# A conditioned attention layer and a GRU: q and k projected by 32-token blocks and heads, turned by VectorE's block transposes

## The chip, the cores and the metric

The kernel runs on one core of a Trainium2 chip. The time is device microseconds (us) of one launch, the median over runs. A core has five engines that run side by side and wait for each other through semaphores: TensorE (PE) multiplies matrices and writes its results to PSUM, eight banks of 128 partitions by 512 float32; VectorE (DVE), ScalarE (ACT) and GpSimd (POOL) compute elementwise on SBUF, the working memory; SyncE (SP) starts DMA transfers. POOL reads and writes SBUF alone here. Everything is float32.

## The reference, cut to what matters

```python
# x (16, 256, 512), cond (16, 512); 16 heads of 32; T = 256 tokens, B = 16
def attention(x, emb, W_emb, b_emb, g_norm, W_qkv, g_q, g_k, W_out):
    scale, shift = jnp.split(emb @ W_emb + b_emb, 2, axis=-1)
    xn = rms_norm(x, g_norm) * (1.0 + scale) + shift
    q, k, v = heads_of(xn @ W_qkv)                  # each (b, h, n, d)
    q, k = rms_norm(q, g_q), rms_norm(k, g_k)       # over d, per head
    attn = softmax(einsum('bhqd,bhkd->bhqk', q, k) * d ** -0.5)
    o = einsum('bhqk,bhkd->bhqd', attn, v)          # back to (b, n, 512)
    return o + o @ W_out

def gru(h, inputs, W_ih, W_hh, b_ih, b_hh):         # one step for each token
    gi, gh = x_t @ W_ih + b_ih, h @ W_hh + b_hh
    r, z = sigmoid(i_r + h_r), sigmoid(i_z + h_z)
    n = tanh(i_n + r * h_n)
    h = (1 - z) * n + z * h

x = x + attention(x, cond, ...)
x = x + gru(cond, x, ...)
```

## The kernel before

The kernel has two stages. The first, the attention of 16 batches, takes about a third of the span; the second is the GRU, 256 steps one after another, and the change doesn't touch its instructions.

**Order.** PE, DVE, ACT and POOL execute in the order in which the source issues instructions (`manual_schedule`, L699); only SP's DMA queue is ordered by a planner. A wait on an engine therefore holds everything that the source issues behind it on that engine.

**Slots.** The attention runs as a hand-made software pipeline (L783 to L788). For each batch b there are four slots, one for each group g of four heads. Each slot starts with `logits` of (b, g), and beside it works on three other things: the exponentials of this group, the end of the group before (`prev`), and a piece of the projection for the next batch m = b+1. In a slot
- `logits` (L302) gives PE eight matmuls 128x256 into the PSUM banks lg0 to lg3, one bank for each head;
- `maxima` (L330, DVE, 4 instructions) and `exps` (L334, ACT, 8) make the unnormalized attn from those banks; `normalize` (L344) takes a reciprocal on DVE and scales the eight halves on POOL, the scale being ready at the end of the slot, so that POOL works at the start of the next;
- `turn(prev)` (L368) transposes attn of the group before on PE, 32 blocks, into the same banks lg0 to lg3, in two halves: lg0 and lg1 first, lg2 and lg3 second. Each half needs its banks read by this slot's exponentials and attn from POOL;
- `put_turned` (L384) copies those banks to SBUF, by letters: "v" a whole bank on DVE, "a" on ACT, "s" a bank on DVE in two halves;
- `weigh(prev)` (L394) multiplies with v, 8 matmuls of 256 columns, into a bank named in the call; `put_weighed` (L410) copies the result o to `oT` on ACT.

**Projection.** `project(b, n, s, ks, a)` (L237) computes q, k or v (s = 0, 1, 2) for token half n (128 tokens) into one bank: for each of four chunks k of the 512 inputs, four matmuls of 32 tokens by 512 columns, each in its own strip of 32 partitions. In PSUM a partition is a token and a column is (head, d). The profile records each of these float32 matmuls twice. Per batch there are 6 such projections; the slots issue them in pieces: slot 0 makes q of half 0 and starts k of half 0, slot 1 ends it and makes q of half 1, slot 2 k of half 1 and the start of v, slot 3 v. Banks A, X, Y, Z hold them, and o in turn.

**From projection to qkT.** `square` (L252, ACT) and `sum_heads` (L260, DVE) give sums of squares per head, `Rsqrt.first` (L158; one DVE step and Ln, Exp on ACT) and `Rsqrt.second` (L165; three small DVE steps) the reciprocal root. `norm_qk` (L268, DVE, two instructions 128x512) scales q and k into SBUF. As logits need d in the partitions, `turn_qk` (L281) transposes both on PE, 16 blocks for each token half, to two PSUM banks, and `put_qk` (L288) copies these to `qkT` while it multiplies by g_q or g_k (`g_cols`; the factor 32 ** -0.5 is in g_q), one bank on DVE and one on ACT. In slot 3 both token halves are turned, one before and one after attn's transposes. `qkT` is one buffer.

**The next x.** `norm_first` (squares on ACT), `norm_apply` (DVE, writes `xs`), `turn_x` (PE, into Y and Z in slot 0) and `put_x` (DVE, in the first batches ACT too) make `xnT`, two batches ahead. `norm_apply` also issues a DMA for a later x.

**Weights.** `we` (W_emb, 2 MB) and later `wih` (W_ih, 3 MB) share a buffer, tag w_a; `wih` is loaded at the start, 16 DMAs on SP behind x of the first batches, W_qkv and W_out, as soon as `we` has been used (L746). `whh` takes the place of W_qkv after the last projection. `last_batch` (L641) does the attention of the last batch with nothing beside it.

Of the kernel before, what the change touches and what calls it, by code (L numbers as in the profile page):

```python
# [8 lines left out]
F32 = mybir.dt.float32  # L9
AF = mybir.ActivationFunctionType  # L10
# [9 lines left out]
def kernel(  # L20
# [42 lines left out]
    ada_s = const.tile([P, KC, B], F32, name="ada_s")  # L63
    g_cols = const.tile([P, 2], F32, name="g_cols")

# [22 lines left out]

    rows = p1.tile([14, P], F32, tag="qkn", name="rows", bufs=4)
    nc.scalar.dma_start(rows[0:8, :], b_emb.rearrange("(m c) -> m c", c=P))  # L90
# [14 lines left out]

    we = wpool.tile([P, KC, 2 * D], F32, tag="w_a", name="we")
    wq = wpool.tile([P, KC, 3 * D], F32, tag="w_b", name="wq")
# [25 lines left out]

    qkT = p1.tile([P, 2, NG, T], F32, name="qkT")
    qT, kT = qkT[:, 0], qkT[:, 1]

# [42 lines left out]
    def norm_first(b, parts=range(NT)):  # L179
        if parts[0] == 0:  # L180
            batches[b].ssx = small.tile([P, NT], F32, tag="ssx", name=f"ssx_{b}")
            batches[b].rs = Rsqrt(batches[b].ssx, D, NT, f"x{b}")
            if b != 2:
                batches[b].xs = p1.tile([P, NT, D], F32, tag="xs", name=f"xs_{b}")
        for n in parts:

            squares = batches[b].xs[:, n, :] if b != 2 else spare(f"squares_{n}")
            nc.scalar.activation(
                squares, x_tiles[b][:, n, :], AF.Square,
                accum_out=batches[b].ssx[:, n : n + 1],  # L190
            )
# [5 lines left out]
    def norm_apply(b, rstd):  # L197
        if b == 2:
            batches[b].xs = p1.tile([P, NT, D], F32, tag="xs", name=f"xs_{b}")
        for n in range(NT):  # L200
            nc.vector.tensor_scalar(
                batches[b].xs[:, n, :], x_tiles[b][:, n, :], rstd[:, n : n + 1],
                None, ALU.mult,
            )
# [14 lines left out]
    def turn_x(b, banks):  # L219
        tps = [tile_ps(f"tpx_{b}_{r}", banks[r], (P, KC, NT, QR)) for r in range(R)]  # L220
        for c in range(KC):
            for n in range(NT):
                turn_block(
                    [tp[:, c, n, :] for tp in tps], batches[b].xs[:, n, c * P : (c + 1) * P]
                )
        return tps
# [10 lines left out]
    def project(b, n, s, ks, a):  # L237
# [12 lines left out]
        return a  # L250

    def square(b, n, s, a):  # L252
        if b == 0:
            sq = spare(f"sq_{b}_{n}_{s}")
        else:
            sq = p1.tile([P, D], F32, tag="sq", name=f"sq_{b}_{n}_{s}")
        nc.scalar.activation(sq, a, AF.Square)
        return sq
# [3 lines left out]

    def put_v(b, n, a, engine=nc.scalar):
        if n == 0:
            batches[b].v = p2.tile([P, NT, D], F32, tag="v", name=f"v_{b}")
        (nc.scalar.copy if engine is nc.scalar else nc.vector.tensor_copy)(batches[b].v[:, n, :], a)

    def norm_qk(b, n, accs, rstd):  # L268
        out = []
        for s in range(2):  # L270
            qk = p1.tile([P, H, DH], F32, tag="qkn", name=f"qkn_{b}_{n}_{s}", bufs=4)
            nc.vector.tensor_tensor(
# [7 lines left out]

    def turn_qk(b, n, normed, banks):  # L281
        tps = [tile_ps(f"tpqk_{b}_{n}_{r}", banks[r], (P, 2, NG, QR)) for r in range(R)]
        for s in range(2):
            for c in range(NG):
                turn_block([tp[:, s, c, :] for tp in tps], normed[s][:, c * P : (c + 1) * P])
        return tps

    def put_qk(n, r, tps, engine):  # L288

        dst = qkT[:, :, :, n * P + QR * r : n * P + QR * r + QR]  # L290
        if engine is nc.scalar:
            for s in range(2):
                nc.scalar.activation(dst[:, s], tps[r][:, s], AF.Copy, scale=g_cols[:, s : s + 1])
        else:
            g = g_cols.unsqueeze(2).unsqueeze(3).to_broadcast([P, 2, NG, QR])
            nc.vector.tensor_tensor(dst, tps[r], g, ALU.mult)

# [18 lines left out]
    def add_logits(w, heads):  # L316
        for i in heads:
            w.lg[i] = ps_lg.tile([P, NT, T], F32, tag=f"lg{i}", name=f"lg_{w.b}_{w.g}_{i}")
        for n in range(NT):
            for i in heads:  # L320
                r = slice(i * DH, (i + 1) * DH)
                nc.tensor.matmul(  # L322
                    w.lg[i][:, n, :],
                    qT[r, w.g, n * P : (n + 1) * P],
                    kT[r, w.g, :],
                    start=True,
                    stop=True,
                )
# [100 lines left out]
    def slot0(b, w, prev, st):  # L429
        m = b + 1  # L430
        if b == 0:


            v = project(b, 1, 2, range(KC), "X")
            put_x(1, 0, st.tpx)
# [4 lines left out]
            norm_apply(2, batches[2].rs.second())  # L440
            put_v(b, 1, v)
            st.q = project(m, 0, 0, range(KC), "A")
            tp = turn_x(2, "YZ")
# [3 lines left out]
            st.s0.add(0, st.s0.square(0, st.q))  # L447
            st.k = project(m, 0, 1, (0, 1), "X")
            normalize(w)
            return  # L450
        put_v(b, 1, st.v1)
        st.q = project(m, 0, 0, range(KC), "A")
        tpx = turn_x(b + 2, "YZ") if b + 2 < B else None
# [16 lines left out]
    def slot1(b, w, prev, st):  # L470
        m = b + 1
        project(m, 0, 1, (2, 3), st.k)
        st.q1 = project(m, 1, 0, (0, 1, 2), "Z")
        maxima(w, range(HG))
# [3 lines left out]
        put_turned(prev, "vasa")  # L478
        project(m, 1, 0, (3,), st.q1)
        st.s0.add(1, sq)  # L480
        if b + 3 < B:
            norm_first(b + 3, (0,))
        st.s0.rs.first()
        st.s1 = Stats(m, 1)
        st.sq = st.s1.square(0, st.q1)
        weigh(prev, "Y")
        put_weighed(prev)
        st.rstd = st.s0.rs.second()
        normalize(w)

    def slot2(b, w, prev, st):
        m = b + 1
        k = project(m, 1, 1, range(KC), "Y")
        maxima(w, range(HG))
        st.qk0 = norm_qk(m, 0, (st.q, st.k), st.rstd)
        st.v0 = project(m, 0, 2, (0,), "A")
        exps(w, range(HG))
        st.s1.add(0, st.sq)
        sq = st.s1.square(1, k)
        turn(prev)  # L500
        put_turned(prev, "vasa")
        project(m, 0, 2, (1,), st.v0)
        st.s1.add(1, sq)
        if b + 3 < B:
            norm_first(b + 3, (1,))
        st.s1.rs.first()
        if b + 3 < B:
            batches[b + 3].rs.first()
        weigh(prev, "X")
        put_weighed(prev)  # L510
        if b == 0:
# [9 lines left out]
        st.accs = (st.q1, k)  # L521
        st.rstd = st.s1.rs.second()
        normalize(w)

    def slot3(b, w, prev, st):
# [3 lines left out]
        maxima(w, range(HG))  # L529
        qk1 = norm_qk(m, 1, st.accs, st.rstd)  # L530
        tq0 = turn_qk(m, 0, st.qk0, "ZY")
        if b + 3 < B:
            rstd = batches[b + 3].rs.second()
        put_v(m, 0, st.v0, nc.vector)
        exps(w, range(HG))
        put_qk(0, 0, tq0, nc.vector)
        put_qk(0, 1, tq0, nc.scalar)
        turn(prev)
        put_turned(prev, "vava")

        tq1 = turn_qk(m, 1, qk1, "AZ")
        project(m, 1, 2, (3,), st.v1)
        put_qk(1, 0, tq1, nc.vector)
        put_qk(1, 1, tq1, nc.scalar)
        if b + 3 < B:
            norm_apply(b + 3, rstd)
        normalize(w)
        weigh(prev, "Y")
        put_weighed(prev)
# [149 lines left out]
    with tc.manual_schedule(engines=ORDERED):  # L699
# [29 lines left out]
        nc.vector.tensor_copy(cols, tp[:, :14])  # L729
        nc.vector.tensor_scalar(g_cols[:, 0:1], cols[:, 12:13], DH ** -0.5, None, ALU.mult)  # L730
        nc.vector.tensor_copy(g_cols[:, 1:2], cols[:, 13:14])
        load_x(2)
# [44 lines left out]
        put_v(0, 0, v)
        put_qk(0, 0, tq0, nc.vector)
        put_qk(0, 1, tq0, nc.scalar)
        put_qk(1, 0, tq1, nc.vector)  # L780
        put_qk(1, 1, tq1, nc.scalar)

# [233 lines left out]
```

## Time and profile before

| | us |
|---|---|
| median of three runs | 1729.38 (1729.19 to 1732.28) |
| profiled execution, its own time | 1729.55 |
| its span in the profile | 1727.6 |
| attention of batches 0 to 14 (first logits at 32.8, first of the last batch at 573.1) | 540.3 |
| granted TensorE clock | 1.00 |

Busy time of the groups around the change:

| group | count | busy us | mean ns |
|---|---|---|---|
| qkv, PE matmuls 128x512 (L243) | 3072 | 354.7 | 596 |
| tpqk, PE transposes of q and k (L217) | 512 | 22.1 | 226 |
| tpa, PE transposes of attn (L217) | 2048 | 78.9 | 225 |
| qkT copies on ACT 128x256 (L293) | 64 | 27.4 | 487 |
| qkT copies on DVE 128x512 (L296) | 32 | 22.0 | 686 |
| qkn on DVE 128x512 (L272) | 64 | 40.9 | 681 |
| v copies on DVE / ACT 128x512 (L266) | 15 / 17 | 10.2 / 10.7 | 683 / 629 |
| attn scaled on POOL 128x256 (L349) | 510 | 234.1 | 482 |

How to read it: "busy" is the time in which an engine executes, and instructions of one engine overlap at their ends, so that a group's busy time divided by its count is less than the mean duration of one. PE matmuls of four strips run beside each other. An engine's idle time counts only where the chain that ends last goes through it. A line such as `128*32 128x512` gives the rows and columns of PE that are in use, and then partitions by elements of the result.

### The profile page before, as it was taken

To read this page: it belongs to the slowest core of one execution; us is meant where nothing else is said; L and a number is where in the kernel's file an instruction comes from. 1 tells how busy PE (TensorE), PEld (TensorE's weight loads), DVE (VectorE), ACT (ScalarE), POOL (GpSimd) and SP (SyncE) were. 2 spreads that over 40 slices of the span, in tenths; PEclk is the share of its full clock that TensorE was granted. 3 is DMA by queue.
4 is the path that set the end of the run, shared out by engine and by line. 5 is a ranking of instruction groups with operands and counts; after the bars stand their busy time and mean duration, and the time that the engine had idled before them with its cause. 6 is when DMAs were issued, how large, how long until landed. Compare 5 with 4: busy or idle time off the path is not lost.

```text
span 1727.6 us, 95661 instructions
## 1 busy us (share of the span) xinstructions
PE 1709.4 (99%) x42876; PEld 1262.6 (73%) x42876; DVE 1058.1 (61%) x3326; ACT 734.4 (43%) x2678; POOL 317.2 (18%) x773
## 2 busy tenths in 40 slices
PE   8999999999999999999999999999999999999998
PEld 4444444444444698888888888888888888888887
DVE  4777777777776755555555555555555555555554
ACT  4777777777777622222222222222222222222222
POOL 0444334443344400000000000000000000000000
PEclk9999999999999999999999999999999999999999
DMA  8100000000000310000000000000000000000000
GB/s 284 46 14 14 17 24 14 14 15 21 8 2 2 76 34 17 17 22 22 17 17 23 22 17 17 19 24 18 17 18 22 21 17 16 17 10 11 10 16 15
DMA packets 50505, 44.36 MB, mean 26 GB/s; under 512 B 10195, under 2 KB 43327, under 8 KB 50095
## 3 DMA queue, kind: packets, MB, share of 16 engines
q1 hardware_dynamic: 49959, 38.21, 8.0%
q8 instruction: 336, 5.51, 1.3%
q14 instruction: 74, 0.61, 0.1%
q10 hardware_dynamic: 136, 0.04, 0.0%
HBM read 29.79 MB, written 8.39 MB: 22 GB/s over the span
## 4 chain that ended last, share of the span: by engine, by line
PE 84%; DVE 6%; ACT 4%; POOL 2%; DMA 2%; issue 1%; SPq 0%; DVEq 0%; ACTq 0%; POOLq 0%
PE gr L601 25%; PE gz L601 18%; PE qkv L243 13%; PE gn L601 13%; PE o L810 6%; PE tpa L217 2%; POOL attn L349 2%; PE lg L322 2%; DVE attnT L380 2%; ACT attn L338 2%; PE o L402 2%; DVE xnT L235 2%; DMA wih<-in_L_cond_W_ih_dram 1%; PE tpqk L217 1%; DVE ssqk L261 1%
## 5 line engine op out<-in xcount | busy, mean ns | idle before, releaser
L243 PE MATMUL qkv<-wq,xnT 128*32 128x512 f32 x3072 | 354.7, 596 | 4.7 <-ACT oT L413 3.5
L349 POOL TENSOR_SCALAR attn<-attn,rden 128x256 f32<-128x256 f32 x510 | 234.1, 482 | 361.0 <-DVE rden L346 235.1
L932 ACT ACTIVATE r<-trr 128x64 f32<-128x64 f32 x256 | 65.5, 256 | 515.2 <-DVE trr L859 513.4
L601 PE MATMUL gr<-wih,xT 128*32 128x256 f32 x4096 | 268.9, 379 | 0.0
L338 ACT ACTIVATE attn<-lg,neg 128x256 f32<-128x256 f32 x512 | 234.9, 486 | 51.9 <-DVE neg L332 34.3
L859 DVE STREAM_TRANSPOSE trr<-gr 128x128 f32<-128x128 f32 x256 | 81.2, 317 | 274.6 <-PE gr L601 274.6
L243 PEld LDWEIGHTS qkv<-wq,xnT 128*32 128x32 f32 x3072 | 88.3, 109 | 186.4 <-issue 166.4
L938 ACT ACTIVATE n<-n 128x64 f32<-128x64 f32 x256 | 65.7, 257 | 307.9 <-DVE n L937 306.4
L601 PEld LDWEIGHTS gr<-wih,xT 128*32 128x32 f32 x4096 | 135.3, 110 | 83.0
L332 DVE TENSOR_REDUCE neg<-lg 128x2 f32<-128x512 f32 x256 | 159.2, 683 | 26.0 <-PE lg L322 24.8
L859 DVE STREAM_TRANSPOSE trh<-gn 128x128 f32<-128x128 f32 x256 | 81.2, 317 | 116.8 <-PE gn L601 116.8
L810 PE MATMUL o<-oT,wo 128*32 128x256 f32 x1920 | 148.1, 379 | 0.0
L968 POOL TENSOR_TENSOR y<-xT,padded 128x64 f32<-128x64 f32 x128 | 41.2, 322 | 534.2 <-DVE padded L966 534.2
L601 PE MATMUL gr<-whh,padded 128*32 128x128 f32 x4096 | 136.1, 273 | 2.7 <-DVE padded L966 1.4
L601 PEld LDWEIGHTS gr<-whh,padded 128*32 128x32 f32 x4096 | 114.8, 109 | 30.4 <-DVE padded L966 29.9
L601 PE MATMUL gz<-wih,xT 128*32 128x128 f32 x4096 | 135.8, 273 | 0.0
L601 PE MATMUL gn<-whh,padded 128*32 128x128 f32 x4096 | 135.6, 273 | 0.0
L601 PE MATMUL gz<-whh,padded 128*32 128x128 f32 x4096 | 135.6, 273 | 0.0
L601 PE MATMUL gr<-whh,h 128*16 128x128 f32 x4064 | 134.7, 273 | 0.7 <-DVE h L966 0.4
L601 PE MATMUL gz<-whh,h 128*16 128x128 f32 x4064 | 134.6, 273 | 0.0
L601 PE MATMUL gn<-whh,h 128*16 128x128 f32 x4064 | 134.6, 273 | 0.0
L601 PEld LDWEIGHTS gz<-wih,xT 128*32 128x32 f32 x4096 | 117.9, 110 | 21.4
(120 smaller groups left out, 2471.6 us busy)
## 6 DMA issues: line engine op xcount, KB each, us to landing
x<-in_x_dram SPq DMA_DIRECT2D x16, 512.0 KB, 3.5
xin<-in_x_dram SPq DMA_DIRECT2D x256, 32.0 KB, 2.6
out_dram<-osb SPq DMA_DIRECT2D x248, 32.0 KB, 1.7
wq<-in_L_cond_W_qkv_dram SPq DMA_DIRECT2D x4, 768.0 KB
wih<-in_L_cond_W_ih_dram SPq DMA_DIRECT2D x16, 192.0 KB, 6.6
whh<-in_L_cond_W_hh_dram SPq DMA_DIRECT2D x16, 192.0 KB, 6.4
we<-in_L_cond_W_emb_dram SPq DMA_DIRECT2D x4, 512.0 KB, 4.8
wo<-in_L_cond_W_out_dram SPq DMA_DIRECT2D x1, 1024.0 KB, 16.9
```

What stands on the lines that cost most here:

```text
L217: nc.tensor.transpose(dst[r], src[q], ident[q, q])
L235: nc.vector.tensor_scalar(dst, tps[r][:, c], a, s, ALU.mult, ALU.add)
L243: nc.tensor.matmul(a[32 * j : 32 * j + 32, :], batches[b].xnT[:, k, n * P + 32 * j : n * P + 32 * j + 32], wq[:, k, s * D : (s + 1) * D], ...
L332: nc.vector.tensor_reduce(w.neg[:, i, :], w.lg[i], AX.X, ALU.max, negate=True)
L338: nc.scalar.activation(a[:, n, :], w.lg[i][:, n, :], AF.Exp, bias=w.neg[:, i, n : n + 1], accum_out=w.den[:, i, n : n + 1],)
L349: engine.tensor_scalar(w.attn[i][:, n, :], w.attn[i][:, n, :], w.rden[:, i, n : n + 1], 1.0, ALU.mult, ALU.mult,)
L601: nc.tensor.matmul(dst[32 * j : 32 * j + rows], stationary, w[:, k, :].rearrange("p (g j c) -> p j g c", g=3, c=P)[:, j, first::2][:, : ds ...
L810: nc.tensor.matmul(acc[32 * j : 32 * j + 32, :], w[:, k, P * j + 32 * m : P * j + 32 * m + 32], rhs, start=(k == 0), stop=(k == KC - 1),)
L859: nc.vector.transpose(tr.rearrange("p q s b -> p (q s b)"), gate)
L932: nc.scalar.activation(r, turned("r", t, gr[:, 0, :])[:, :, s, :], AF.Sigmoid)
L938: nc.scalar.activation(n, n, AF.Tanh)
L968: (nc.gpsimd if t + 1 < T else nc.vector).tensor_tensor(y[:, :, tl * B : (tl + 1) * B], xTs[grp][:, :, ti, :], h, ALU.add)
```

## The change

It replaces the way in which q and k reach `qkT`.

- A new `project_qk` takes the place of `project` for q and k. One bank now holds 64 tokens of q and k together: partition strip j holds 32 tokens of head j of every group of four heads, and the two column halves i are two blocks of 32 tokens. So there are twice as many matmuls with half the columns each, and the weight columns that one reads are eight pieces of 32.
- `turn_qk` uses VectorE's transpose, which turns each block of 32x32 by itself, from SBUF straight to `qkT`, one instruction of 128x512 for each bank. `qkT` has two buffers, one for each of two batches.
- `put_qk` is gone. g_q, g_k and 32 ** -0.5 are multiplied into one column `g_col`, and `scale_q` scales q alone in place, on POOL (in the first batch on ACT).
- In slot 2 the transposes for token half 0, in slot 3 those for half 1 follow `norm_qk`; the second part of the reciprocal root for half 1 moves from slot 2 to slot 3. v of half 0 is copied by ACT, later. In slot 1 and slot 2 `weigh` and `put_weighed` stand ahead of a square or the next `Rsqrt.first`. In slot 3 o goes to bank Z, and a bank of attn is copied in halves.
- `xs` becomes a part of the buffer w_a behind `we`; `wih` is loaded in slot 1 of batch 13 in the source, and SP's planner puts the first 8 of its 16 DMAs early.
- In the first batch three of four chunks of v for token half 1 are projected ahead of the first logits.

```diff
+    def project_qk(b, n, m, ks, a):
+        if isinstance(a, str):
+            a = tile_ps(f"qk_{b}_{n}_{m}", a)
+        w = wq[:, :, 0 : 2 * D].rearrange("p k (s g j d) -> p k j s g d", s=2, j=HG, d=DH)
+        for k in ks:
+            for i in range(2):
+                t = n * P + 64 * m + 32 * i
+                for j in range(HG):
+                    nc.tensor.matmul(
+                        a[32 * j : 32 * j + 32, i * T : (i + 1) * T],
+                        batches[b].xnT[:, k, t : t + 32],
+                        w[:, k, j],
+                        start=(k == 0 and i == 0),
+                        stop=(k == KC - 1),
+                        skip_group_check=True,
+                    )
+        return a
...
-    def turn_qk(b, n, normed, banks):
-        tps = [tile_ps(f"tpqk_{b}_{n}_{r}", banks[r], (P, 2, NG, QR)) for r in range(R)]
-        for s in range(2):
-            for c in range(NG):
-                turn_block([tp[:, s, c, :] for tp in tps], normed[s][:, c * P : (c + 1) * P])
-        return tps
-
-    def put_qk(n, r, tps, engine):
...
+    def turn_qk(b, n, normed):
+        if n == 0:
+            batches[b].qkT = p1.tile([P, 2 * NG, T], F32, tag="qkT", name=f"qkT_{b}", bufs=2)
+        for m, a in enumerate(normed):
+            t = n * P + 64 * m
+            nc.vector.transpose(
+                batches[b].qkT[:, :, t : t + 64].rearrange("p h (i t) -> p i h t", i=2), a
+            )
+
+    def scale_q(b, n, engine=nc.gpsimd):
+        q = batches[b].qkT[:, 0:NG, n * P : (n + 1) * P]
+        if engine is nc.scalar:
+            nc.scalar.activation(q, q, AF.Copy, scale=g_col)
+        else:
+            engine.tensor_scalar(q, q, g_col, 1.0, ALU.mult, ALU.mult)
...
     def slot1(b, w, prev, st):
...
+        elif b + 3 == B:
+            load_rows(wih, w_ih)
         st.s0.rs.first()
         st.s1 = Stats(m, 1)
-        st.sq = st.s1.square(0, st.q1)
         weigh(prev, "Y")
         put_weighed(prev)
+        st.sq = st.s1.square(0, st.q1)
         st.rstd = st.s0.rs.second()
         normalize(w)

     def slot2(b, w, prev, st):
         m = b + 1
-        k = project(m, 1, 1, range(KC), "Y")
+        k = project_qk(m, 1, 1, range(KC), "Y")
         maxima(w, range(HG))
-        st.qk0 = norm_qk(m, 0, (st.q, st.k), st.rstd)
+        qk0 = norm_qk(m, 0, (st.q, st.k), st.rstd)
+        turn_qk(m, 0, qk0)
+        scale_q(m, 0)
         st.v0 = project(m, 0, 2, (0,), "A")
         exps(w, range(HG))
-        st.s1.add(0, st.sq)
         sq = st.s1.square(1, k)
         turn(prev)
         put_turned(prev, "vasa")
         project(m, 0, 2, (1,), st.v0)
+        st.s1.add(0, st.sq)
         st.s1.add(1, sq)
         if b + 3 < B:
             norm_first(b + 3, (1,))
+        weigh(prev, "X")
+        put_weighed(prev)
         st.s1.rs.first()
         if b + 3 < B:
             batches[b + 3].rs.first()
-        weigh(prev, "X")
-        put_weighed(prev)
...
     def slot3(b, w, prev, st):
...
-        qk1 = norm_qk(m, 1, st.accs, st.rstd)
-        tq0 = turn_qk(m, 0, st.qk0, "ZY")
+        turn_qk(m, 1, norm_qk(m, 1, st.accs, st.s1.rs.second()))
+        scale_q(m, 1)
+        exps(w, range(HG))
+        turn(prev)
+        put_turned(prev, "vasa")
+        put_v(m, 0, st.v0)
+        project(m, 1, 2, (3,), st.v1)
         if b + 3 < B:
-            rstd = batches[b + 3].rs.second()
-        put_v(m, 0, st.v0, nc.vector)
-        exps(w, range(HG))
-        put_qk(0, 0, tq0, nc.vector)
-        put_qk(0, 1, tq0, nc.scalar)
-        turn(prev)
-        put_turned(prev, "vava")
-
-        tq1 = turn_qk(m, 1, qk1, "AZ")
-        project(m, 1, 2, (3,), st.v1)
-        put_qk(1, 0, tq1, nc.vector)
-        put_qk(1, 1, tq1, nc.scalar)
-        if b + 3 < B:
-            norm_apply(b + 3, rstd)
+            norm_apply(b + 3, batches[b + 3].rs.second())
         normalize(w)
-        weigh(prev, "Y")
+        weigh(prev, "Z")
         put_weighed(prev)
...
+        turn_qk(0, 0, qk0)
+        scale_q(0, 0, nc.scalar)
         norm_first(2)
-        qk1 = norm_qk(0, 1, accs[1], s1.rs.second())
-        tq0 = turn_qk(0, 0, qk0, "AX")
-        tq1 = turn_qk(0, 1, qk1, ("lg2", "lg3"))
+        turn_qk(0, 1, norm_qk(0, 1, accs[1], s1.rs.second()))
+        put_v(0, 0, v)
+        scale_q(0, 1, nc.scalar)
         st.tpx = turn_x(1, "YZ")
+        st.v1 = project(0, 1, 2, (0, 1, 2), "X")
```

More of the change, by code (lines that the diff above doesn't have):

```diff
@@ L63 @@
     ada_s = const.tile([P, KC, B], F32, name="ada_s")
-    g_cols = const.tile([P, 2], F32, name="g_cols")
+    g_col = const.tile([P, 1], F32, name="g_col")
     b_rows = const.tile([P, 4, P], F32, name="b_rows")
@@ L86 @@
     ps = ctx.enter_context(tc.tile_pool(name="ps", bufs=1, space=PSUM))
-    rows = p1.tile([14, P], F32, tag="qkn", name="rows", bufs=4)
+    rows = p1.tile([14, P], F32, tag="qkn", name="rows", bufs=2)
     nc.scalar.dma_start(rows[0:8, :], b_emb.rearrange("(m c) -> m c", c=P))
@@ L104 @@
     load_x(0)
-    we = wpool.tile([P, KC, 2 * D], F32, tag="w_a", name="we")
+    w_a = wpool.tile([P, KC * 3 * D], F32, name="w_a")
+    we = w_a[:, 0 : KC * 2 * D].rearrange("p (k n) -> p k n", k=KC)
+    xs = w_a[:, KC * 2 * D : KC * 2 * D + NT * D].rearrange("p (n d) -> p n d", n=NT)
+    wih = w_a.rearrange("p (k n) -> p k n", k=KC)
     wq = wpool.tile([P, KC, 3 * D], F32, tag="w_b", name="wq")
@@ L128, in load_small @@
                 nc.sync.dma_start(h0P[r, q, :], h0T[32 * q : 32 * q + 32, j, :])
-    qkT = p1.tile([P, 2, NG, T], F32, name="qkT")
-    qT, kT = qkT[:, 0], qkT[:, 1]
     def load_rows(dst, w):
@@ L182, in norm_first @@
             batches[b].rs = Rsqrt(batches[b].ssx, D, NT, f"x{b}")
-            if b != 2:
-                batches[b].xs = p1.tile([P, NT, D], F32, tag="xs", name=f"xs_{b}")
         for n in parts:
-            squares = batches[b].xs[:, n, :] if b != 2 else spare(f"squares_{n}")
+            squares = xs[:, n, :] if b != 2 else spare(f"squares_{n}")
             nc.scalar.activation(
@@ L197, in norm_apply @@
     def norm_apply(b, rstd):
-        if b == 2:
-            batches[b].xs = p1.tile([P, NT, D], F32, tag="xs", name=f"xs_{b}")
         for n in range(NT):
             nc.vector.tensor_scalar(
-                batches[b].xs[:, n, :], x_tiles[b][:, n, :], rstd[:, n : n + 1],
+                xs[:, n, :], x_tiles[b][:, n, :], rstd[:, n : n + 1],
                 None, ALU.mult,
@@ L223, in turn_x @@
                 turn_block(
-                    [tp[:, c, n, :] for tp in tps], batches[b].xs[:, n, c * P : (c + 1) * P]
+                    [tp[:, c, n, :] for tp in tps], xs[:, n, c * P : (c + 1) * P]
                 )
@@ L261, in sum_heads, with put_v @@
         nc.vector.tensor_reduce(ss[:, s, :], sq.rearrange("p (h d) -> p h d", d=DH), AX.X, ALU.add)
-    def put_v(b, n, a, engine=nc.scalar):
+    def put_v(b, n, a):
         if n == 0:
             batches[b].v = p2.tile([P, NT, D], F32, tag="v", name=f"v_{b}")
-        (nc.scalar.copy if engine is nc.scalar else nc.vector.tensor_copy)(batches[b].v[:, n, :], a)
+        nc.scalar.copy(batches[b].v[:, n, :], a)
     def norm_qk(b, n, accs, rstd):
@@ L270, in norm_qk @@
         for s in range(2):
-            qk = p1.tile([P, H, DH], F32, tag="qkn", name=f"qkn_{b}_{n}_{s}", bufs=4)
+            qk = p1.tile([P, H, DH], F32, tag="qkn", name=f"qkn_{b}_{n}_{s}", bufs=2)
             nc.vector.tensor_tensor(
@@ L279, in norm_qk @@
         return out
-    def turn_qk(b, n, normed, banks):
-        tps = [tile_ps(f"tpqk_{b}_{n}_{r}", banks[r], (P, 2, NG, QR)) for r in range(R)]
-        for s in range(2):
-            for c in range(NG):
-                turn_block([tp[:, s, c, :] for tp in tps], normed[s][:, c * P : (c + 1) * P])
-        return tps
-    def put_qk(n, r, tps, engine):
-        dst = qkT[:, :, :, n * P + QR * r : n * P + QR * r + QR]
+    def turn_qk(b, n, normed):
[8 more added lines that the diff above has]
+        q = batches[b].qkT[:, 0:NG, n * P : (n + 1) * P]
         if engine is nc.scalar:
-            for s in range(2):
-                nc.scalar.activation(dst[:, s], tps[r][:, s], AF.Copy, scale=g_cols[:, s : s + 1])
-        else:
-            g = g_cols.unsqueeze(2).unsqueeze(3).to_broadcast([P, 2, NG, QR])
-            nc.vector.tensor_tensor(dst, tps[r], g, ALU.mult)
+            nc.scalar.activation(q, q, AF.Copy, scale=g_col)
+        else:
+            engine.tensor_scalar(q, q, g_col, 1.0, ALU.mult, ALU.mult)
     class Group:
@@ L323, in add_logits @@
                     w.lg[i][:, n, :],
-                    qT[r, w.g, n * P : (n + 1) * P],
-                    kT[r, w.g, :],
+                    batches[w.b].qkT[r, w.g, n * P : (n + 1) * P],
+                    batches[w.b].qkT[r, NG + w.g, :],
                     start=True,
@@ L431, in slot0 @@
         if b == 0:
-            v = project(b, 1, 2, range(KC), "X")
+            project(b, 1, 2, (3,), st.v1)
             put_x(1, 0, st.tpx)
@@ L440, in slot0 @@
             norm_apply(2, batches[2].rs.second())
-            put_v(b, 1, v)
-            st.q = project(m, 0, 0, range(KC), "A")
+            put_v(b, 1, st.v1)
+            st.q = project_qk(m, 0, 0, range(KC), "A")
             tp = turn_x(2, "YZ")
@@ L447, in slot0 @@
             st.s0.add(0, st.s0.square(0, st.q))
-            st.k = project(m, 0, 1, (0, 1), "X")
+            st.k = project_qk(m, 0, 1, (0, 1), "X")
             normalize(w)
@@ L451, in slot0 @@
         put_v(b, 1, st.v1)
-        st.q = project(m, 0, 0, range(KC), "A")
+        st.q = project_qk(m, 0, 0, range(KC), "A")
         tpx = turn_x(b + 2, "YZ") if b + 2 < B else None
@@ L461, in slot0 @@
         put_turned(prev, "vava")
-        st.k = project(m, 0, 1, (0, 1), "X")
+        st.k = project_qk(m, 0, 1, (0, 1), "X")
         if tpx:
@@ L471, in slot1 @@
         m = b + 1
-        project(m, 0, 1, (2, 3), st.k)
-        st.q1 = project(m, 1, 0, (0, 1, 2), "Z")
+        project_qk(m, 0, 1, (2, 3), st.k)
+        st.q1 = project_qk(m, 1, 0, (0, 1, 2), "Z")
         maxima(w, range(HG))
@@ L478, in slot1 @@
         put_turned(prev, "vasa")
-        project(m, 1, 0, (3,), st.q1)
+        project_qk(m, 1, 0, (3,), st.q1)
         st.s0.add(1, sq)
@@ L521, in slot2 @@
         st.accs = (st.q1, k)
-        st.rstd = st.s1.rs.second()
         normalize(w)
@@ L729 @@
         nc.vector.tensor_copy(cols, tp[:, :14])
-        nc.vector.tensor_scalar(g_cols[:, 0:1], cols[:, 12:13], DH ** -0.5, None, ALU.mult)
-        nc.vector.tensor_copy(g_cols[:, 1:2], cols[:, 13:14])
+        nc.vector.scalar_tensor_tensor(
+            g_col, cols[:, 12:13], DH ** -0.5, cols[:, 13:14], ALU.mult, ALU.mult
+        )
         load_x(2)
@@ L743 @@
         nc.sync.dma_start(wo, w_out.rearrange("(k p) n -> p k n", p=P))
-        wih = wpool.tile([P, KC, 3 * D], F32, tag="w_a", name="wih")
-        load_rows(wih, w_ih)
         for c in range(KC):
@@ L753 @@
             for i in range(2):
-                accs[n][i] = project(0, n, i, ks, accs[n][i])
+                accs[n][i] = project_qk(0, n, i, ks, accs[n][i])
         v = project(0, 0, 2, range(KC), "lg0")
@@ L771 @@
         s1.rs.first()
+        turn_qk(0, 0, qk0)
+        scale_q(0, 0, nc.scalar)
         norm_first(2)
-        qk1 = norm_qk(0, 1, accs[1], s1.rs.second())
-        tq0 = turn_qk(0, 0, qk0, "AX")
-        tq1 = turn_qk(0, 1, qk1, ("lg2", "lg3"))
+        turn_qk(0, 1, norm_qk(0, 1, accs[1], s1.rs.second()))
+        put_v(0, 0, v)
+        scale_q(0, 1, nc.scalar)
         st.tpx = turn_x(1, "YZ")
[L777 to L781, printed above, removed]
+        st.v1 = project(0, 1, 2, (0, 1, 2), "X")
         prev = None
```

## The prediction

> **What bounds the kernel now.** I read the page's busy shares first, then the chain of waits over the first 120 us, then timelines of single stages, then the groups by shape.
>
> ```profile
> PE 1709.4 (99%) x42876; PEld 1262.6 (73%) x42876; DVE 1058.1 (61%) x3326; ACT 734.4 (43%) x2678; POOL 317.2 (18%) x773
> ```
>
> PE is busy almost everywhere, but that share doesn't tell whether it waits inside a stage. The starts of the logits (L322) in the timeline do. From batch 1 on the four slots of a batch last 9.12, 8.50, 8.81 and 9.50 us, 35.93 together, within 0.02 in all 14 batches. All of them hold logits, six products (8 records each: four matmuls of 512 columns in two passes), the transposes of attn, and o; so the differences are what to look at. The chain shows them (start us, us, what):
>
> ```profile
> 44.56 4.43 PE qkv L243 x40
> 48.99 0.69 PE tpa L217 x16
> ...
> 52.23 0.49 ACT sq L257
> 52.72 0.49 ACT oT L413
> 53.20 0.04 issue
> 53.25 4.50 PE qkv L243 x40
> ...
> 61.82 4.43 PE qkv L243 x40
> 66.25 0.65 PE tpqk L217 x16
> 66.89 0.99 PE tpa L217 x32
> 67.88 0.50 PE tpqk L217 x16
> 68.38 1.00 PE qkv L243 x8
> 69.38 0.86 PE o L402 x16
> 70.24 1.08 PE lg L322 x16
> 71.32 3.57 PE qkv L243 x32
> ```
>
> Slot 3 is PE from end to end, and two groups of tpqk stand in it. Slot 2 begins with a wait: ACT squares q before it copies o out of the bank that the next projection needs. The same in a later slot 2, with the wait in brackets:
>
> ```profile
> 303.63 0.58 ACT L257 ACTIVATE sq<-qkv 128x512 f32<-128x512 f32 x1
> 304.11 0.58 ACT L413 COPY oT<-o 128x256 f32<-128x256 f32 x1
> 304.75 0.16 PEld L243 LDWEIGHTS qkv<-wq,xnT 128*32 128x32 f32 x8 [0.64 <-ACT oT L413]
> ```
>
> Slot 0 has another limit. In the last slot 0, which has no tpx, PE still waits for the exponentials before the second half of attn's transposes, and the slot is 9.12 as ever:
>
> ```profile
> 542.33 0.51 ACT L338 ACTIVATE attn<-lg,neg 128x256 f32<-128x256 f32 x1
> 542.98 0.71 PE L217 MATMUL tpa<-ident,attn 64*128 64x64 f32 x15 [0.35 <-ACT attn L338]
> ```
>
> That half can start 5.77 us after the slot's logits begin. In slots 1 to 3 PE itself only reaches it at 6.01 (logits 1.08, five products 4.43, first half 0.50), so there PE sets the pace, with 0.24 to spare.
>
> **The price of each operation** (by shape: busy us, mean ns):
>
> ```profile
> L402 PE MATMUL o<-attnT,v 128*32 128x256 f32 x1024 | 67.3, 379 | 0.1
> L719 PE MATMUL ps_emb<-we,h0T 128*16 128x256 f32 x32 | 2.5, 384 | 1.4 <-DMA we<-in_L_cond_W_emb_dram 1.0 <-DVE h0T L713 0.3
> L824 DVE STREAM_TRANSPOSE xT<-xin 128x512 f32<-128x512 f32 x32 | 22.4, 702 | 0.4 <-issue 0.2
> L380 DVE COPY attnT<-tpa 128x512 f32<-128x512 f32 x98 | 64.7, 684 | 62.2 <-ACT sq L257 37.2 <-PE tpa L217 23.2 <-ACT attn L338 1.8
> ```
>
> *q and k in 32-token blocks.* A batch's 64 matmuls of 512 columns become 128 of 256. Four that share a pass start together, each runs in two passes. By the trace's starts a 512 pass follows the last after 0.430 us, a 256 pass (L402, and L601's gr, whose 256 columns come in two pieces) after 0.216. So 64 passes replace 32 per batch: 64x0.216 against 32x0.430, +0.06 us. What is new is that the moving columns come in eight pieces of 32; only L719 reads like that, and its second pass follows after 0.226. Low end +0.06 us a batch, high end 64x0.010 more, 10 us over 16 batches. I take the low end, because L719's extra 0.010 always follows a wait for DMA, as a first pass after idle does.
>
> [...]
>
> *PE's transposes go.* 32 tpqk per batch: by the chain slot 3 is 0.65+0.99+0.50+1.00 from tpqk to the end of v; without them tpa and v take 1.14+0.99, as the chain has them in slot 2. Slot 3 falls by 1.01, from 9.50 to 8.49.
>
> *The wait in slot 2 goes.* o's copy now stands ahead of the square: ACT starts it at 303.63 instead of 304.11, it ends at 304.21, PE's logits at 304.44. So 8.81 becomes 8.50. The square behind it ends near 304.8, before the first maximum allows an exponential (305.3).
>
> *VectorE.* Per batch it loses two copies of qkT (L296, 686 ns) and one of v, and gains four transposes 128x512. L824 is the nearest row: 702 ns, 0.61 from start to start. The destination differs (runs of 32 in eight heads, there runs of 16). Bounds: 0.60, the cadence of L380, and twice 0.61. I take 0.61.
> Walk of slot 3 (us after its logits start): maxima 1.16 to 3.55, the three small steps of the reciprocal root, now placed here, to 4.3, two qkn to 5.5, two transposes to 6.7, then attnT: bank 0 until 7.4, the first half of bank 2 until 7.73. PE is ready for o at 7.50 and needs that half at its third matmul: 0.27 lost. Slot 3 is 8.76, not 8.49. Behind these wait the next xs (needed by PE 4.65 into slot 0) and rden, 1.05 into slot 0; POOL then ends at 5.0, PE asks from 5.15. Maxima may start at 1.16, so that cover is thin: 0.1.
> In slot 2 transposes end at 5.96 and tpa's first half reaches VectorE at 6.15: hidden, with 0.48 to spare before o would wait.
>
> *POOL scales q.* Two 128x512 per batch; L349 does 128x256 in 482 ns, so 0.96 each, near 6.1 to 7.1 in slot 2 and 6.7 to 7.7 in slot 3. POOL is done with attn at 4.9 and idle until the next rden; if it weren't, logits of the next slot 0 would wait, 0.8 further on. ACT loses four L293 (487 ns) and gains a v copy (629): less work, none on the path.
>
> *SP's queue.* w_ih's 16 DMAs leave the start: 8 now stand behind the small loads, 8 in batch 13's slot 1 behind all x. There they wait for PE, and behind them stands only w_hh, which waits for the last projection anyway. 3.1 MB some 80 us ahead of use: nothing on the path. The loads of x 2 and x 3 come sooner; PE waited for neither.
>
> *The first batch.* v's three products move ahead of the logits, where PE would wait for VectorE. From 30.03: tpx to 30.7, v to 33.35; transposes of the second half end near 33.0, ACT's scaling 33.7; logits 33.4 to 34.3 (before: 32.84 to 33.91); last v product and q to 38.7, tpx 39.3; k needs v's bank, copied after the exponentials, 39.75; next logits 41.6 instead of 43.42: -1.8.
>
> **Sum.** Batches 1 to 14: 9.12+8.50+8.50+8.76+0.06 = 34.94, -0.99 each, -13.9. Batch 0: -1.8 and slots 1 to 3 -0.95. The last batch's first transposes wait for POOL, whose rden comes some 0.2 later: +0.2. Together -16.45. The profiled execution took 1729.55 (span 1727.6 and 1.95 around it), 0.17 above the median of the three runs: 1713.1.
>
> **Rivals.** A difference under 0.2% (3.5 us) can't be told from none.
> 1. More: slot 3 doesn't stall (8.49) and the start gains more, under 1708. For it: L402's third matmul may overlap the wait. 0.09.
> 2. Less: L719's 0.226 is the real pass (+10), or slot 3 loses 0.3 to 0.8 us more to VectorE's queue: 1719 to 1726. For it: only L719 shows this reading. Against: a wait precedes each. 0.13.
> 3. It doesn't do what it says: the wait for PE's transposes becomes one for VectorE's of equal length, slot 3 near 9.5, start unchanged: 1726 to 1733. Against: the walk leaves 0.7 us. 0.05.
> 4. Slower: the transposes of VectorE are dear. Each extra d over 0.61 delays o by 2d in slot 3 and by 2d-0.48 in slot 2; the gain of 1.09 a batch is gone at d = 0.39 (1.00 us from start to start), slower by more than 0.2% from 1.06; at twice the row 15x1.96 = 29 us, 1742. For it: no row has this destination. Against: L824's also scatters. 0.10.
>
> The forecast's own range, 1708 to 1719, gets 0.63. Of rivals 1 and 2 the nearer parts are taken in: 1706 to 1723. Faster 0.63+0.13+0.09 = 0.85, same 0.05, slower 0.10.
>
> **What would show it.** No tpqk; logits 9.12, 8.50, 8.50, 8.76 apart; passes of the new projection 0.216 apart; the new transposes near 0.70 us; o in slot 3 released by VectorE's copy, late by some 0.3; no wait for oT at the start of slot 2. A pass of 0.23 or more, a transpose over 1 us, or a POOL that releases logits would make it wrong.

## The result and the profile after

The changed kernel is slower: 1749.10 us, median of four runs (1748.43 to 1751.17), against 1729.59 (1729.19 to 1732.28) of the kernel before in the same measurement. The ratio is 1.0112, 95% interval 1.0094 to 1.0129. The profiled execution took 1748.59, its span is 1746.8. Forecast were 1713.1, with a range of 1706 to 1723.

The four slots of a batch, by the starts of the logits, as the prediction counted them (batches 1 to 14):

| us | slot 0 | slot 1 | slot 2 | slot 3 | sum |
|---|---|---|---|---|---|
| before | 9.12 | 8.50 | 8.81 | 9.50 | 35.93 |
| forecast | 9.12 | 8.50 | 8.50 | 8.76 | 34.88 + 0.06 |
| after | 9.11 | 8.53 | **10.91** | 8.77 | 37.32 |

Three of four slots are where they were forecast; slot 2 alone is 2.4 us longer than forecast, in each of 15 batches. The page of the changed kernel shows little of this in its busy times; PE is still at 98%.

```profile
PE 1706.8 (98%) x44412; PEld 1312.5 (75%) x44412; DVE 1071.1 (61%) x3357; ACT 716.4 (41%) x2631; POOL 336.6 (19%) x803
```

The chain of waits does (start us, us, what). The stretch is one slot 2, whose logits began at 88.80:

```profile
89.88 3.59 PE qk L260 x64
93.47 0.86 PE qkv L241 x8
94.33 0.69 PE tpa L215 x16
95.01 1.34 DVE attnT L400 x3
96.36 0.60 DVE ssqk L280
...
97.04 0.60 ACT sq L276
97.64 0.48 ACT attnT L400
...
98.17 1.55 PE o L422 x16
```

No tpqk is left, and no wait for oT at the start of slot 2: the next projection follows the logits at once (89.88). But from 95.01 to 98.17 the chain leaves PE: it runs through DVE's copies of attnT, DVE's sum `ssqk`, ACT's square and ACT's copy of attnT, before o can start. Only slot 3 shows the small loss that was forecast: in the same view its o, at 107.35, takes 0.28 us longer than that of a slot 1.

```profile
87.94 0.86 PE o L422 x16
...
107.35 1.14 PE o L422 x16
```

The groups by shape show the same (busy us, mean ns | idle us before, and what ended it):

```profile
L422 PE MATMUL o<-attnT,v 128*32 128x256 f32 x1024 | 79.9, 382 | 25.9 <-ACT attnT L400 25.5
...
L306 DVE STREAM_TRANSPOSE qkT<-qkn 128x512 f32<-128x512 f32 x64 | 41.4, 685 | 0.0
L276 ACT ACTIVATE sq<-qk 128x512 f32<-128x512 f32 x64 | 39.7, 620 | 40.3 <-DVE ssqk L280 38.8 <-PE qk L260 1.5
```

ACT's square waits 38.8 us for `ssqk`, 15 times 2.6; o waits 25.5 us for ACT's attnT. Before, o waited 0.1 us. The new work itself is as cheap as forecast: transposes 685 ns (forecast from a row of 702), and L260's passes (the new `project_qk`) start 0.216 us apart.

Why a square should wait for a sum is seen in the timeline of a later slot 2 of the changed kernel:

```profile
356.62 1.35 DVE L400 COPY attnT<-tpa 128x512 f32<-128x512 f32 x3 [0.21 <-PE tpa L215]
...
357.89 0.68 DVE L280 TENSOR_REDUCE ssqk<-sq 128x16 f32<-128x512 f32 x1
358.66 0.60 ACT L276 ACTIVATE sq<-qk 128x512 f32<-128x512 f32 x1 [2.60 <-DVE ssqk L280]
359.15 1.07 ACT L400 COPY attnT<-tpa 128x512 f32<-128x512 f32 x2
...
359.78 1.55 PE L422 MATMUL o<-attnT,v 128*32 128x256 f32 x16 [1.70 <-ACT attnT L400]
```

`square` takes its output from the tag sq, which has one buffer. The square of `st.q1` (slot 1) lies in it until DVE has summed it. (The code and this text go on calling the two banks of a token half q and k; after the change each holds 64 tokens of both.) The diff moves that sum, `st.s1.add(0, st.sq)` in slot 2, from ahead of the square of k to behind `put_turned`, and so behind DVE's copies of attnT. The square of k can't overwrite the buffer until then, and ACT's own two copies of attnT stand in ACT's order behind the square. ACT is ready at about 356.1 and idles for 2.60 us.

### The profile page after: what moved, and what is told of

The parts are those of the page before. It is cut to its first block, busy times and chain, and to the rows that moved or that the text cites. A ratio compares the mean times of both kernels' runs of the same rounds, so it can differ in the third digit from the quotient of the medians.

```text
span 1746.8 us, 98734 instructions
## 1 busy us (share of the span) xinstructions
PE 1706.8 (98%) x44412; PEld 1312.5 (75%) x44412; DVE 1071.1 (61%) x3357; ACT 716.4 (41%) x2631; POOL 336.6 (19%) x803
## 4 chain that ended last, share of the span: by engine, by line
PE 92%; DVE 4%; ACT 2%; DMA 1%; issue 1%; ACTq 0%; POOL 0%; DVEq 0%; SPq 0%
PE gr L616 25%; PE gz L616 18%; PE gn L616 13%; PE qk L260 12%; PE o L821 6%; PE qkv L241 5%; PE o L422 4%; PE lg L342 4%; PE tpa L215 4%; DVE attnT L400 1%; DMA x<-in_x_dram 1%; DVE ssqk L280 1%; ACT sq L276 1%; PE tpx L215 0%; ACT attnT L400 0%
## 5 line engine op out<-in xcount | busy, mean ns | idle before, releaser
L616 PE MATMUL gr<-w_a,xT 128*32 128x256 f32 x4096 | 268.9, 379 | 0.0
L260 PE MATMUL qk<-wq,xnT 128*32 128x256 f32 x4096 | 236.7, 381 | 1.3 <-DVE xnT L233 1.1
L616 PEld LDWEIGHTS gr<-w_a,xT 128*32 128x32 f32 x4096 | 135.4, 110 | 82.8
L260 PEld LDWEIGHTS qk<-wq,xnT 128*32 128x32 f32 x4096 | 125.4, 110 | 93.5 <-ACT oT L433 9.3
L979 POOL TENSOR_TENSOR y<-xT,h 128x64 f32<-128x64 f32 x127 | 40.8, 321 | 501.0 <-DVE h L977 501.0
L616 PE MATMUL gz<-w_a,xT 128*32 128x128 f32 x4096 | 135.9, 273 | 0.0
```

What stands on the lines that cost most here:

```text
L260: nc.tensor.matmul(a[32 * j : 32 * j + 32, i * T : (i + 1) * T], batches[b].xnT[:, k, t : t + 32], w[:, k, j],  start=(k == 0 and i == 0), ...
L616: nc.tensor.matmul(dst[32 * j : 32 * j + rows], stationary, w[:, k, :].rearrange("p (g j c) -> p j g c", g=3, c=P)[:, j, first::2][:, : ds ...
L979: (nc.gpsimd if t + 1 < T else nc.vector).tensor_tensor(y[:, :, tl * B : (tl + 1) * B], xTs[grp][:, :, ti, :], h, ALU.add)
```

## The experiments

**The sum at its old place, or late in the kernel before.** The theory was that the moved sum with the single buffer makes the slot long; the rival, that VectorE's transposes, which now stand in slot 2, do. The first four runs had a second buffer, two other places for the sum, and the kernel before with only that one line moved. (The letters in the expectations are those of each set of runs; in the second set, from e5 on, A is this theory, B and C are two on slot 3.) All four compute the same as the kernel they start from.

`e1_second_square` gives the square of q its own place in the spare part of w_a, except in the last two batches, where `wih` lies there:

```diff
     def square(b, n, s, a):
         if b == 0:
             sq = spare(f"sq_{b}_{n}_{s}")
+        elif (n, s) == (1, 0) and b < 14:
+            sq = w_a[:, KC * 2 * D + NT * D : KC * 2 * D + NT * D + D]
         else:
```

> The changed kernel, but q's squares of token half 1 go to a piece of the w_a buffer that is free until w_ih's last rows come, so the next squares needn't wait for their sum; for batches 14 and 15, where w_ih already fills that piece, the one shared buffer stays. Theory A (in slot 2 ACT's squares of k wait for VectorE's sum of q's squares, which the change moved behind the copies of attn, and ACT's own copies of attn stand behind these squares): 13 of 15 slots 2 fall from 10.91 to 8.5, 13 x 2.4 = 31 us less than 1749.1, so 1718. Rival B (VectorE's new transposes crowd slot 2 and make the copies late whatever the squares do): slot 2 stays over 10, 1740 to 1749. Rival C (the start costs it, first logits 1.4 us later than before): at most 2 us change.

Measured: 1725.77 (1724.17 to 1726.93), ratio to the kernel before 0.9970 (0.9958 to 0.9981); slots 9.11, 8.53, **8.53**, 9.16 to 9.33, and in the last two batches 10.91 and 8.77 as after. Slot 2 falls by the whole 2.38. Slot 3 rises by 0.3 to 0.55 in 13 batches, which was not expected: some 6 us of the 7.8 that the run missed (more on slot 3 below). Most of the rest is in the start: the first logits of the profiled execution come at 36.32, 2.0 later than after's.

`e2_sum_after_norm` has the sum right behind `norm_qk`, ahead of the transposes:

```diff
         qk0 = norm_qk(m, 0, (st.q, st.k), st.rstd)
+        st.s1.add(0, st.sq)
         turn_qk(m, 0, qk0)
...
         project(m, 0, 2, (1,), st.v0)
-        st.s1.add(0, st.sq)
         st.s1.add(1, sq)
```

> The changed kernel with one line moved: the sum of q's squares of token half 1 stands right behind the two qkn in slot 2, ahead of VectorE's transposes. One buffer for squares as before. Theory A: ACT's squares wait for nothing, all VectorE work behind the sum is 0.61 later, so o may wait some 0.1 to 0.2; slot 2 at 8.6 to 8.7, 15 x 2.25 = 34 us less, so 1715. Rival B: VectorE's queue in slot 2 is as long as it was, slot 2 stays over 10, 1740 to 1749. Rival C: at most 2 us change.

Measured: 1721.96 (1720.12 to 1722.65), ratio 0.9944 (0.9929 to 0.9959); slots 9.11, 8.53, **8.69**, 9.06. Slot 2 is repaired but for 0.16, as expected: the sum (0.67, and 0.59 from its start to the next) pushes the transposes back from 4.76 to 5.35 us after the slot's logits. Again slot 3 is longer than after, by 0.29. Over 15 batches that is 4.4 of the 7 us that the run missed; the start has a part in the rest, with first logits at 35.36 where after has 34.27.

`e3_before_sum_late` is the kernel before with one line moved:

```diff
         exps(w, range(HG))
-        st.s1.add(0, st.sq)
         sq = st.s1.square(1, k)
         turn(prev)
         put_turned(prev, "vasa")
         project(m, 0, 2, (1,), st.v0)
+        st.s1.add(0, st.sq)
         st.s1.add(1, sq)
```

> The kernel before with one line moved as in the change: in slot 2 the sum of q's squares stands behind attn's copies; nothing else of the change. Theory A: the squares of k and ACT's copies of attn behind them wait here too, slot 2 grows from 8.81 to 11.2, 15 x 2.4 = 36 us more than 1729.6, so 1765. Rivals B and C (transposes, start): no VectorE transposes and the old start, so within 3 us of 1729.6.

Measured: 1765.46 (1765.23 to 1766.79), ratio 1.0199 (1.0184 to 1.0214); slot 2 is 11.20 instead of 8.81, 2.39 more, with no transposes of VectorE in the kernel at all. The chain of that run has the same links in the same order as the changed kernel's:

```profile
96.84 1.34 DVE attnT L380 x3
98.18 0.60 DVE ssqk L261
...
98.87 0.60 ACT sq L257
99.46 0.48 ACT attnT L380
...
99.99 1.55 PE o L402 x16
```

`e4_sum_old_place` puts the sum of the changed kernel back to its old place, which is now behind the transposes:

```diff
         exps(w, range(HG))
+        st.s1.add(0, st.sq)
         sq = st.s1.square(1, k)
         turn(prev)
...
-        st.s1.add(0, st.sq)
         st.s1.add(1, sq)
```

> The changed kernel with the moved line put back to its old place, ahead of attn's copies and behind VectorE's transposes. Theory A: VectorE reaches the sum only after the transposes, 5.9 us into slot 2, so ACT's squares start at 6.6 instead of 5.8, its first copy of attn ends at 7.8 and its second at 8.3, where PE would start o at 7.5: slot 2 at 9.2 to 9.3, 15 x 1.65 = 25 us less than 1749.1, so 1724. If the place didn't matter and only the new transposes did (rival B), 1740 to 1749. Rival C: at most 2 us change.

Measured: 1727.40 (1724.13 to 1728.12), ratio 0.9975 (0.9966 to 0.9984); slot 2 is 9.32. So the old place would not have been free either: the sum then ends behind 1.28 of qkn and 1.29 of transposes, and the square still waits, by 1.01 us in the timeline. The theory of the moved sum holds, and the transposes have a share through it, as they make the old place late. Ahead of them the sum costs slot 2 0.16; with a buffer of its own, nothing.

**Slot 3.** In e1 and e2, where slot 2 was short (8.53 and 8.69), slot 3 was longer than after's 8.77. The timeline of e1's slot 3 shows the three small root steps (L169, L170, L172), which the change moved from the end of slot 2 to behind slot 3's maxima:

```profile
274.99 3.65 POOL L371 TENSOR_SCALAR attn<-attn,rden 128x256 f32<-128x256 f32 x8 [2.53 <-ACT y_qk L164]
...
277.71 0.51 DVE L169 SCALAR_TENSOR_TENSOR u_qk<-y_qk 128x32 f32<-128x32 f32 x1
278.25 0.42 DVE L170 TENSOR_TENSOR u_qk<-u_qk,m_qk 128x32 f32<-128x32 f32 x1
278.71 0.19 DVE L172 SCALAR_TENSOR_TENSOR y_qk<-u_qk,y_qk 128x32 f32<-128x32 f32 x1
```

The first two take 0.51 and 0.42 us while GpSimd scales attn (274.99 to 278.64), where 0.19 is usual (so all three at 266.00, before GpSimd starts at 266.93), and behind them stand qkn, the transposes and the copies that o waits for. In the changed kernel slot 2's stall hid this: ACT's square delayed everything up to o and the next logits, but not rden, so GpSimd was nearly done when VectorE came to the steps (it scales from 361.31 to 364.96 in one such slot; the steps start at 364.83 and take 0.18, 0.19 and 0.19). The theories for the second set were that the steps' place costs time (B), and that GpSimd's work stretches them (C).

`e5_steps_back` is e2 with the steps at the end of slot 2, and with `weigh` and `put_weighed` behind `Rsqrt.first` again, both as the kernel before has them:

```diff
         if b + 3 < B:
             norm_first(b + 3, (1,))
-        weigh(prev, "X")
-        put_weighed(prev)
         st.s1.rs.first()
         if b + 3 < B:
             batches[b + 3].rs.first()
+        weigh(prev, "X")
+        put_weighed(prev)
...
+        st.rstd = st.s1.rs.second()
         normalize(w)
...
-        turn_qk(m, 1, norm_qk(m, 1, st.accs, st.s1.rs.second()))
+        turn_qk(m, 1, norm_qk(m, 1, st.accs, st.rstd))
```

> The changed kernel with the sum of q's square behind the division, as in e2_sum_after_norm, and the three steps of the reciprocal root put back at the end of slot 2, ahead of rden, as the kernel before has them (and with them ScalarE's Ln and Exp ahead of the copy of oT). It computes the same. Theory B (these three steps, which the change moved behind slot 3's maxima, are what the transposes and then o wait for in slot 3: 0.66 us when GpSimd is idle, 0.94 in the run of e2): slot 3 falls from 9.06 to 8.5, slot 2 stays at 8.7, 14.5 times 0.55 = 8 us less than that run's 1722.0, so 1714. Rival: slot 3 is long because VectorE's transposes stand in it, wherever the steps are: slot 3 stays at 9.0 and the time at 1722. Second rival: the steps delay rden and the maxima, and slot 3 gains nothing because the exponentials come later: 1720 or more.

Measured: 1713.27 (1713.02 to 1713.97), ratio 0.9903 (0.9889 to 0.9916); slots 9.11, 8.53, 8.69, **8.50**. It beats both kernels, and theory B holds to the tenth. Its chain stays on PE from slot 2 to slot 3 where the changed kernel's left it, between tpa and o:

```profile
269.19 1.15 PE tpa L215 x32
270.33 0.99 PE qkv L241 x8
271.33 1.02 PE o L422 x16
272.35 1.08 PE lg L342 x16
273.43 4.43 PE qkv L241 x40
```

`e8_half_scaling` is e1 with only two of four heads scaled by GpSimd at the end of slot 2. It leaves out the division for the other two, and so doesn't compute the same:

```diff
         st.accs = (st.q1, k)
-        normalize(w)
+        nc.vector.reciprocal(w.rden, w.den)
+        for i in (0, 1):
+            for n in range(NT):
+                nc.gpsimd.tensor_scalar(
+                    w.attn[i][:, n, :], w.attn[i][:, n, :], w.rden[:, i, n : n + 1], 1.0,
+                    ALU.mult, ALU.mult,
+                )
```

> e1_second_square with half of GpSimd's scaling of attn in slot 2 left out (heads 2 and 3 of that group stay undivided), so GpSimd is done 1.8 us sooner, before VectorE reaches the three root steps. Theory C (in that run the steps take 0.51, 0.42 and 0.2 to 0.42 us in place of 0.19 each because GpSimd works on SBUF at the same time): they go back to 0.19 each and slot 3 falls from 9.16 to 9.33 to some 8.8, 13 times 0.45 = 6 us, 1720. Rival (GpSimd has nothing to do with it, the steps are slow for their place): durations and slot 3 stay, 1725.8.

Measured: 1719.78 (1718.68 to 1719.95), ratio 0.9938 (0.9925 to 0.9952); slot 3 falls from e1's 9.16 to 9.33 to 8.77. The steps are back at their usual length in the timeline of this run, as GpSimd ends at 273.99:

```profile
272.15 1.84 POOL L551 TENSOR_SCALAR attn<-attn,rden 128x256 f32<-128x256 f32 x4 [2.53 <-ACT y_qk L164]
...
274.87 0.18 DVE L169 SCALAR_TENSOR_TENSOR u_qk<-y_qk 128x32 f32<-128x32 f32 x1
275.09 0.19 DVE L170 TENSOR_TENSOR u_qk<-u_qk,m_qk 128x32 f32<-128x32 f32 x1
```

Theory C holds too. The runs make a series: the steps, from the start of the first to qkn, take no time in slot 3 (e5), 0.67 us (after and e8), 0.96 (e2), 1.06 or 1.22 (e1, by batch), and slot 3 is 8.50, 8.77, 9.06, 9.16 and 9.32. Behind the first 0.4 us, which have cover, a microsecond of these steps is a microsecond of the slot.

`e6_square_and_steps` joins the second buffer and the steps' old place (the last two batches take the buffer from a free tile of x):

```diff
         elif (n, s) == (1, 0) and b < 14:
             sq = w_a[:, KC * 2 * D + NT * D : KC * 2 * D + NT * D + D]
+        elif (n, s) == (1, 0):
+            sq = p2.tile([P, NT, D], F32, tag="x", name=f"sq_{b}")[:, 0, :]
```

> The changed kernel with a second buffer for the square of q of the second half, as in e1_second_square, but for the last two batches too (there in a free tile of x), and the three root steps back at the end of slot 2. It computes the same. Theory A with B: slots 9.11, 8.53, 8.53 and 8.5, 34.67 against 37.33 of the changed kernel, 15 times 2.66 = 40 us less than 1749.1, plus 1 to 3 for the low clock of the first 30 us that the runs of the first call had: 1709 to 1713, and faster than e5_steps_back by 2 to 3 us. If one of the two theories is short: 1718 (slot 3 stays above 9).

Measured: 1713.14 (1712.81 to 1713.69), ratio 0.9901 (0.9886 to 0.9917); slots 9.11, 8.53, 8.53, 8.64. The total is just above the expected range, and the gain of 2 to 3 us over e5 is missed: what slot 2 gains, 0.16, slot 3 gives back, 0.14. The trace shows where. In this run the sum of q still stands behind the copies of attn, and the steps and rden follow it. So slot 3's maxima start 1.61 us after its logits instead of 1.16 in e5, and its last exponential ends at 6.00 instead of 5.61. In the chain tpa takes 1.27 us there instead of 1.14 in e5. That fits the second rival of e5's expectation, exponentials that come later, with ACT as the next limit; no run with the steps back varied the sum's place alone.

**The order in slot 1 alone.** `e7_oT_first` is the kernel before with this edit only:

```diff
         st.s1 = Stats(m, 1)
-        st.sq = st.s1.square(0, st.q1)
         weigh(prev, "Y")
         put_weighed(prev)
+        st.sq = st.s1.square(0, st.q1)
```

> The kernel before, with one edit: in slot 1 ScalarE copies oT out of its bank ahead of the square of q, as the changed kernel does. It computes the same. The prediction's step for this edit alone: slot 2 falls from 8.81 to 8.50, 15 times 0.31 = 4.6 us, 1725. Rival: the square then ends too late for VectorE's sum or for the exponentials, and slot 2 stays at 8.8: 1729.6.

Measured: 1726.94 (1724.82 to 1729.14), ratio 0.9981 (0.9972 to 0.9990). Slot 2 is 8.50 in every batch, with slots 0, 1 and 3 as before, so the step is worth the forecast 0.31 per batch. That the median gained less than 4.6 us lies at the start: the six runs with a mean clock of 0.999 or more have a median of 1725.2, the eleven such runs of the kernel before in this measurement 1729.4. The stretches of this run's profile from 10 to 20 us (the stretch, its length, busy us of PE, PEld, DVE, ACT and POOL with counts, then the granted TensorE clock, the DMA share and GB/s) show a clock near 0.5:

```profile
10.00:15.00 5.00, 3.99 (x36) 1.45 (x40) 2.37 (x8) 1.31 (x4) 0.00 (x0) 0.50 1.03 431
15.00:20.00 5.00, 5.00 (x32) 1.37 (x28) 0.07 (x1) 0.19 (x1) 0.00 (x0) 0.53 1.01 407
```

## Why the prediction was wrong

**The step that failed** is in the part on VectorE, its last sentence: "In slot 2 transposes end at 5.96 and tpa's first half reaches VectorE at 6.15: hidden, with 0.48 to spare before o would wait." The walk counted how long VectorE is busy and left out one line of the diff, the moved sum, and what it releases: the only buffer for squares. With it, slot 2's o waits on ACT, whose square waits on VectorE. The same hole is in "The wait in slot 2 goes", which gave slot 2 its 8.50, and in ACT's "less work, none on the path": here ACT's square and its copy of attn are on the path. The description of the change doesn't name the move; it stands only in the diff. In its place the runs showed 10.91, and one moved line alone, in the kernel before, costs 2.39 a batch (e3).

The account: batches 1 to 14 take 523.1 us, 34.0 more than 14 times the forecast 34.94; all but 0.6 of it is 2.38 a batch (37.32 against 34.94), and most of the 0.6 is one slot 3 of 9.08 and one slot 1 of 8.76. Batch 0 adds 2.8, of it 2.4 in slot 2 and 0.4 in slot 3. The start is 0.9 later than forecast. The 256 steps of the GRU, whose code is the same, take 1.8 less (1108.04 us from the first step's end to the last's, against 1109.84 before). 1713.1 + 34.0 + 2.8 + 0.9 - 1.8 = 1749.0, against 1748.59 of the profiled execution; the 0.2 that was forecast for the last batch didn't come. The shorter GRU is in every run that starts from the changed kernel (1107.9 to 1108.0), and not in e3 and e7 (1109.8); its cause stays open.

**What held.** 
- Passes of 256 columns, read in eight pieces, follow each other after 0.216 us; so the reading in pieces is not what made L719's 0.226, and rival 2's first mechanism is out. Slot 1 is 8.53 instead of 8.50, half of the 0.06 forecast for the batch.
- The transposes take 0.685 us and 0.63 from one start to the next (forecast 0.61), so rival 4's price didn't come. Its sign did, by another mechanism: a dependency, not a price.
- Slot 3 of 8.76, with 0.27 lost to the root steps, the transposes and the copies, was measured at 8.77. But it was right for a slot 2 that stalls. The forecast had GpSimd "done with attn at 4.9", and the steps placed at 3.55 to 4.3 beside it, at their usual length. With a short slot 2 they would have met and taken 9.06 to 9.33 (e1, e2). So even without the failed step the kernel would have stood near 1721 (e1 less 2.4 for each of its two long batches) or 1722 (e2), at the end of the range.
- The wait for oT went, worth 0.31 (e7).
- GpSimd's scaling of q was forecast at 0.96 us, twice a row of half the size; it is 0.69. It has cover in every run, and nothing hangs on it.

**The start.** First logits come at 34.27, forecast 33.4 (32.84 before), second at 42.49, forecast 41.6. The distance between them is right; both are late by 0.9, of which 0.83 is there before the first projection (13.53 against 12.70 us), where PE waits for the last two pieces of W_emb (0.86 and 0.62 us, before 0.43 and 0.61). In other runs with this start they come later still, in e5 at 38.03: of these 3.8 us, 1.6 are there before the first projection (15.10) and 2.2 come behind it, under a granted clock of 0.50 (from 10 to 15 us) and 0.54 (from 15 to 20). But e7, with the start of the kernel before, has both too: first logits at 36.92 against 32.84, the first projection at 14.16. So the change is not the only cause. Whether the change makes it more frequent is open: 30 of 37 runs with the new start and 15 of 46 with the old have a mean clock of 0.998 or less (a short drop hides in 0.999, as in e2's profiled run), but no run varied the start alone.

## What to carry to other kernels

When a diff moves an instruction that only reads, ask which buffer it releases and who writes that buffer next; with one buffer, a late reader holds the writer, and with it all that stands behind the writer on its engine. A moved line deserves a term of the sum even where the moved work itself is small: here a sum of 0.68 us cost 2.4. And a stall can hide the next cost, so a repair is priced by the slot as it will then be: here 0.3 to 0.55 us of the gain was lost again in the slot behind it, until the second line was put back too.

## What the runs showed of the hardware

VectorE's small root steps, which read and write SBUF, took longer beside GpSimd's scaling of attn in SBUF. In e1 the first root step starts beside a busy GpSimd in 13 batches. In seven of them it takes 0.50 us and in one 0.22, and the second step then takes 0.42; in the other five it takes its usual 0.18, and the second 0.35. In e2's timeline the first takes 0.47 (from 277.09, with GpSimd busy until 277.52), and the second, behind GpSimd's end, 0.19. Beside an idle GpSimd the same instructions take 0.18 and 0.19 (e8). The maxima, which read PSUM, don't show it: four take 2.48 us in e1, with GpSimd busy all the while, and 2.48 in e8, where GpSimd stops on the way. The time added is 0.33 us at most (0.51 against 0.18), less than one of GpSimd's instructions takes (0.478 on average in e8). By what mechanism the steps are held up, the runs don't show.

In the profiled executions of all experiments but e3 the granted clock of TensorE falls to 0.50 near the start, at 9.0 to 14.1 us; in the profiles of e3 and of the kernels before and after it is 1.00 there. (Where the profile gives mean clocks of stretches of 5 us alone, starts and lengths are estimated from them, with 0.50 for the low part.) In e5 and e7 it falls, at 9.4 and 9.5, before the last product with W_emb (at 12.27 and 11.33), for whose pieces PE waits between its matmuls; in e1 it falls 2.0 us after that product. It stays there for some 3.4 us (e1, e2), 6.8 (e4, e8) or 10.2 to 10.3 (e5, e6, e7), about one, two or three times the same length. In e7 it lasts from 9.5 to 19.7, and the first logits come 4.1 us later than in the kernel before: 1.5 of that is there before the first projection (14.16 against 12.70), 2.6 comes behind it. Executions of one kernel differ: the eleven of e7 have a mean clock of 0.996 to 1.000. From 5 to 10 us PE is busy for 2.61 to 3.62 us in the seven profiles with the drop, and for 3.73 to 4.11 in the three without it. What brings the drop no run here shows.
